# First attention of a two-layer kernel: another order of the matrix groups within a segment

## The chip, the cores and the metric

The kernel runs on one core of a Trainium2 chip. A core has a matrix engine (TensorE, PE in the profile), three engines for elementwise work (VectorE or DVE, ScalarE or ACT, GpSimd or POOL), a queue that issues transfers (SyncE, SP) and 16 DMA engines. Every engine works through its own queue of instructions in order; semaphores tie the queues together. The metric is the device time of one execution, in microseconds.

## The reference

The program computes two gated layers: `x = x + attention(norm(x)) * silu(ffn(norm(x)))`, twice, on `x` of 4 batches x 512 tokens x 128. The change touches only the first attention, a recurrent one with a memory. With 16 heads of 64 and segments of 64 tokens, cut to what matters:

```python
def step(carry, seg):
    M, Z = carry                               # memory and its normaliser, per head
    q, k, v = ...                              # the segment's 64 tokens, per head
    scores = jnp.einsum('bhid,bhjd->bhij', q, k) * scale
    scores = jnp.where(mask, -jnp.inf, scores)
    att_dot = jnp.einsum('bhij,bhjv->bhiv', softmax(scores), v)
    sq = elu(q) + 1.0
    att_mem = sq @ M / (sq @ swapaxes(Z, -2, -1))
    sk = elu(k) + 1.0
    M_new = M + jnp.einsum('bhld,bhlv->bhdv', sk, v)
    Z_new = Z + sk.sum(axis=-2, keepdims=True)
    att = gate * att_mem + (1.0 - gate) * att_dot
    out = att.reshape(B, LSEG, H * DV) @ Wo
    return ((M_new, Z_new), out)
```

A batch has 8 segments, so there are 32 steps; the memory starts anew with each batch.

## The kernel before

The kernel runs, in this order: the norm and the FFN of the first layer, the first attention (`attn0`, lines 563 to 864), the FFN of the second layer, the second attention. Inside `attn0` the loop `for n in range(nseg)` (line 823) goes over the 32 segments n = 0 to 31. The statements of the loop body fix the order on each engine: what is called earlier stands earlier in the queue of every engine that it uses (only transfers may be issued somewhat earlier or later). The work is software pipelined: while segment n is finished, the scores, keys and queries of n + 1 are prepared and the attention of n - 1 is transposed. The steps, with the tile names that the profile shows:

- `elu_exp(n, w)`: ScalarE takes the exponential (`elu`) and the relu (`up`) of the keys (w = 1) or queries (w = 0) of a segment. `elu(n, w)` (line 679): VectorE makes `min(elu, 1) + up` of them; all three tiles lie in SBUF.
- `scores(n)`: 16 matmuls of 64x64, one per head, spread over the four 64x64 quadrants of TensorE, into PSUM `sc`; VectorE caps and masks them into `E` (line 656). `scores_exp(n)`: ScalarE takes their exponential.
- `memory(n)`: 16 quadrant matmuls of the queries' elu with the memory `mz`, into `mm`; VectorE divides (`rm`, `t`, lines 711 and 712); GpSimd multiplies by the gate (line 731).
- `update(n)`: 16 quadrant matmuls of the keys with the values (`vone`), into `mu`; VectorE adds them to the memory (line 746). It is left out in the last segment of a batch (n % 8 = 7).
- `keys(n)`: four transposes of 128x128 into `pk`; ScalarE copies them to `sk`. It is left out for n % 8 = 7.
- `attend(n)`: 16 quadrant matmuls of `E` with the values, into `dot`; VectorE divides (lines 765, 711, 712) and keeps the largest sums (`sums`, line 768); GpSimd multiplies by the other gate (line 769) and adds the memory's part (line 770).
- `attended(n)`: four transposes into `pa`; ScalarE copies them to `attT` in four instructions.
- `output(h)`: 64 matmul halves into `po` for every four segments, at n % 4 = 1; VectorE multiplies by the gate (line 802), GpSimd adds to `x` (line 803).
- `project(h)`: twelve chunks that make the queries, keys and values of the four segments of group h: eight of q and k (`pp`, 8 matmuls each with 64 columns, evicted by ScalarE to `pj`), four of v (`pv`, evicted to `vt` by ScalarE, by VectorE for the first two groups, and sent to DRAM `vd` by SP). `todo` holds the chunks that are left; `each` of them, four in n = 0 to 2 and three later, are done in a segment, and none from n = 27 on. `values(n)`: SP loads `vone` back from `vd`, two segments ahead.
- `between`: FFN steps of the second layer that are slipped in from n = 18 on.

PSUM has two rings: `wide` (tag `w`, three buffers of two banks), which scores, memory, update, attend and output take in turn, and `narrow` (tag `t`, two buffers of one bank), which chunks, `pk` and `pa` take in turn. A group can start when the buffer that it takes has been evicted. `E`, `elu`, `vt` and the `pj` tiles have two buffers each, `vone` four.

Of the kernel before, what the change touches and what calls it, by code (L numbers as in the profile page):

```python
# [107 lines left out]
class Kernel:  # L108
# [454 lines left out]
    def attn0(self, xnT, g0, stack, psum, between):  # L563
# [25 lines left out]
        def wide(name):  # L589

            return psum.tile([P, 2, S], F32, name=name, tag="w", bufs=3)

        def narrow(name):
            return psum.tile([P, S], F32, name=name, tag="t", bufs=2)
# [44 lines left out]
        def blocks(n, w):  # L639
            s = n % 4  # L640
            return qkv[n // 4][w][:, s * 8 : s * 8 + 8, :]
# [20 lines left out]
        def scores_exp(n):  # L662
            e = seg[n]["e"]
            self.act1(e, e, AF.Exp, scale=1.0 / math.sqrt(DK))

        def last(n):
            return n % 8 == 7

        def elu_exp(n, w):
            t = pool.tile([P, 8, 64], F32, name=f"elu{w}{n}", tag=f"elu{w}")  # L670
            up = pool.tile([P, 8, 64], F32, name=f"up{w}{n}", tag="up")
            self.act1(t, blocks(n, w), AF.Exp)
            self.act1(up, blocks(n, w), AF.Relu)
            seg[n][w] = t, up

        def elu(n, w):

            t, up = seg[n][w]
            self.vec1(nc.vector.scalar_tensor_tensor(t, t, 1.0, up, ALU.min, ALU.add))  # L679
            seg[n][w] = t  # L680

        def turn(n, src, name):

            ps = narrow(f"{name}{n}").rearrange("p (hp c) -> p hp c", hp=4)
            for hp in range(4):
                self.pin(nc.tensor.transpose(
                    ps[:, hp], src[:, 2 * hp : 2 * hp + 2, :].rearrange("d a j -> d (a j)"),
                    self.ident,
                ))
            return ps.rearrange("p hp (x d) -> p hp x d", x=2)  # L690

        def keys(n):
            t = pool.tile([P, 4, 2, DK], F32, name=f"sk{n}", tag="sk")
            self.act1(t, turn(n, seg[n][1], "pk"), AF.Copy)
            seg[n]["sk"] = t

        def values(n):

            for p in range(2):
                src = vd[n // 4][p].rearrange("(s hp r) d -> s r hp d", s=4, hp=4)  # L700
                nc.sync.dma_start(out=vone[n % 4][:, :, p, 0:DK], in_=src[n % 4])

        def heads(ps):

            return ps[:, :, 0 : 4 * (DK + 1)].rearrange("p x (y v) -> p x y v", v=DK + 1)

        def over(t):
            return t.rearrange("p (x hp) y d -> p x (hp y) d", x=2)

        def divided(ps, t, r, sums):  # L710
            self.vec1(nc.vector.reciprocal(r, sums))
            self.vec1(nc.vector.tensor_tensor(t, heads(ps)[:, :, :, 0:DK], bc(r, 3, DK), ALU.mult))  # L712

        def memory(n):


            mz, sq = self.mz[(n % 8 + 1) % 2 + 1 if n % 8 else 0], seg[n][0]
            ps = wide(f"mm{n}")
            for hp in range(4):
                for p in range(2):  # L720
                    for a in range(2):
                        at = (2 * a + hp // 2) * (DK + 1)
                        self.mm1(
                            ps[halves[(a + hp) % 2], p, at : at + DK + 1],
                            lhsT=sq[halves[p], 2 * hp + a, :], rhs=mz[halves[p], hp, a, :],
                            start=True, stop=True,
                        )
            t = seg[n]["t1"] = pool.tile([P, 4, 2, DK], F32, name=f"t1{n}", tag="t1")
            r = pool.tile([P, 2, 4], F32, name=f"rm{n}", tag="rm")
            divided(ps, t.rearrange("p hp y d -> p y hp d"), r, heads(ps)[:, :, :, DK])  # L730
            nc.gpsimd.tensor_mul(t, t, self.gate)  # L731
# [16 lines left out]
        def attend(n):  # L748


            e, v = seg[n]["e"], vone[n % 4]
            ps = wide(f"dot{n}")
            for u in range(2):
                for p in range(2):
                    for hp in (2 * u, 2 * u + 1):
                        for a in range(2):
                            at = (2 * u + p) * (DK + 1)
                            self.mm1(
                                ps[halves[(a + hp) % 2], a, at : at + DK + 1],
                                lhsT=e[halves[a], p, hp, :], rhs=v[halves[a], hp, p, :],  # L760
                                start=True, stop=True,
                            )
            both = pool.tile([P, 2, 2, 4], F32, name=f"rd{n}", tag="rd")
            sums = both[:, 0]
            self.vec1(nc.vector.tensor_scalar_max(sums, heads(ps)[:, :, :, DK], SUM_MIN / 2))
            t = pool.tile([P, 4, 2, DK], F32, name=f"t2{n}", tag="t2")
            divided(ps, over(t), both[:, 1], sums)
            self.vec1(nc.vector.tensor_tensor(self.sums0, both, self.sums0, ALU.max))  # L768
            nc.gpsimd.tensor_mul(t, t, gate2)  # L769
            nc.gpsimd.tensor_add(t, t, seg[n]["t1"])  # L770
            seg[n]["att"] = t

        def attended(n):

            if n % 4 == 0:

                attT[n // 4] = pool.tile([P, 16, 4, 32], F32, name=f"attT{n}", tag="attT")
            ps = narrow(f"pa{n}").rearrange("p (hp c) -> p hp c", hp=4)
            for hp in range(4):
                self.pin(nc.tensor.transpose(  # L780
                    ps[:, hp, :], seg[n]["att"][:, hp].rearrange("i p v -> i (p v)"),
                    self.ident,
                ))
            src = ps.rearrange("p (a u) (h t c) -> p c a u h t", a=2, h=2, c=16)
            dst = attT[n // 4][:, :, n % 4].rearrange("p c (u y t) -> p c u y t", u=2, y=4)
            for h in range(2):
                for a in range(2):
                    self.act1(dst[:, :, :, (a + h) % 2 * 2 + a], src[:, :, a, :, h], AF.Copy)

        def output(h):  # L790
            ps = wide(f"po{h}")
            for c in range(16):
                for p in range(2):
                    self.mm1(
                        ps[:, p, 0:D], lhsT=attT[h][halves[p], c].rearrange("v s x -> v (s x)"),
                        rhs=self.wo[halves[p], c, :],
                        start=(c == 0), stop=(c == 15),
                    )
            two = slice(h * 2, h * 2 + 2)
            gate = g0[h // 2][:, h % 2 * 2 : h % 2 * 2 + 2, :]  # L800
            sg = pool.tile([P, 2, D], F32, name=f"sg{h}", tag="sg")
            self.vec1(nc.vector.tensor_tensor(sg, ps[:, :, 0:D], gate, ALU.mult))
            nc.gpsimd.tensor_add(self.x[:, two, :], self.x[:, two, :], sg)
# [4 lines left out]
        todo = project(0)  # L808
# [14 lines left out]
        for n in range(nseg):  # L823
            if n == 0 or n % 4 == 3:
                todo = project((n + 1) // 4 + 1)
                each = 3 if n else 4
            nxt = n + 1 < nseg
            more = nxt and not last(n + 1)
            if n + 2 < nseg:
                values(n + 2)  # L830
            if more:
                elu_exp(n + 1, 1)
            if nxt:
                scores(n + 1)
            if n % 4 == 1 and n > 4:
                output(n // 4 - 1)
            for chunk in todo[:1]:
                chunk()
            if more:
                elu(n + 1, 1)  # L840
            if nxt:
                scores_exp(n + 1)
            memory(n)
            for chunk in todo[1:2]:
                chunk()
            if nxt:
                elu_exp(n + 1, 0)
            if not last(n):
                update(n)
            if nxt:  # L850
                elu(n + 1, 0)
            for chunk in todo[2:each]:
                chunk()
            todo = todo[each:]
            if more:
                keys(n + 1)
            for f, *args in between.get(n - 0.5, []):
                f(*args)
            attend(n)
            if n:  # L860
                attended(n - 1)
            for f, *args in between.get(n, []):
                f(*args)
        return [lambda: attended(nseg - 1), lambda: output(2 * B - 1)]
# [1392 lines left out]
```

## Time and profile before

| | us |
|---|---|
| three runs | 774.92, 775.71, 767.96 |
| median | 774.92 |
| the profiled execution | 772.95 |
| its span, first to last instruction | 771.1 |
| first attention's loop up to n = 27, 93.66 to 310.09 | 216.43 |
| n = 27 to the last memory group, 310.09 to 335.54 | 25.45 |

| engine | busy in the whole span | busy in 93.66 to 310.09 | busy in 310.09 to 335.54 |
|---|---|---|---|
| PE | 729.7 | 210.29 | 20.06 |
| DVE | 522.8 | 141.68 | 20.86 |
| ACT | 489.6 | 155.23 | 14.97 |
| POOL | 292.7 | 111.68 | 17.05 |

The mean granted clock of TensorE is 0.981. How the profile is read: it shows one execution. Times count from the span's start. In a timeline each row is a run of equal instructions: its start, how long it lasted, engine, line, operation, the tiles written and read, shapes, and how many; a bracket gives the idle time of the engine just before and what ended it. Matmuls are pipelined, so the end of a group of matmuls overlaps the start of the next; the distance between two starts is the time that a group takes. L331 is a helper through which nearly all matmuls go, and L334 one for ScalarE, so groups are told apart by their tiles.

### The profile page before, as it was taken

Reading aid. Unit: us, or ns where it says so; the run is one execution under the profiler, and the core shown is the slowest. Engines: PE = TensorE matmul, PEld = TensorE weight load, DVE = VectorE, ACT = ScalarE, POOL = GpSimd, SP = SyncE. Lnnn points to the kernel's source line nnn. Section 1 sums busy time; section 2 is a strip of 40 time slices with the busy share of each in tenths; the row PEclk is TensorE's granted clock in tenths of the full one; section 3 lists DMA queues with packets and bytes.
Section 4 is the critical chain, followed back from the end, with each engine's and each line's share of the span. In section 5 each row is a group of like instructions: output and inputs, shape, how many; then the busy total and the mean of one; then the engine's idle time right before and its main releaser. Section 6 shows DMA issues by size and latency. Waiting matters only on the chain. (4 is left out here: it accounts for less than half of the span.)

```text
span 771.1 us, 23617 instructions
## 1 busy us (share of the span) xinstructions
PE 729.7 (95%) x10060; PEld 439.4 (57%) x10060; DVE 522.8 (68%) x1133; ACT 489.6 (63%) x793; POOL 292.7 (38%) x340
## 2 busy tenths in 40 slices
PE   8999899999999989889999998999999999999996
PEld 4665677787876858767677775333233433432235
DVE  7776375657558755774356633798897799857864
ACT  4432566768667776653332224899897879889940
POOL 7660045555555435563045030231441244130250
PEclk9999999999999999999999999899999999999997
DMA  7830423223123121100003710849676766749200
GB/s 194 145 84 0 111 85 98 69 61 94 44 75 98 31 83 31 31 3 1 1 0 105 220 47 1 197 153 207 134 210 157 162 140 187 199 113 212 55 16 17
DMA packets 77743, 74.71 MB, mean 97 GB/s; under 512 B 41936, under 2 KB 66800, under 8 KB 74560
## 3 DMA queue, kind: packets, MB, share of 16 engines
q1 hardware_dynamic: 75568, 71.98, 36.0%
q0 software_dynamic: 1488, 0.90, 0.8%
q8 instruction: 81, 1.33, 0.8%
q10 hardware_dynamic: 576, 0.26, 0.1%
q14 instruction: 30, 0.25, 0.1%
HBM read 50.04 MB, written 23.07 MB: 95 GB/s over the span
## 5 line engine op out<-in xcount | busy, mean ns | idle before, releaser
L334 ACT ACTIVATE e<-s 128x1024 f32<-128x1024 f32 x126 | 123.1, 1042 | 24.7 <-PE s L331 23.9
L331 PE MATMUL acc<-e,strip 128*32 128x512 f32 x1008 | 124.9, 604 | 0.3 <-DVE e L1692 0.3
L334 ACT ACTIVATE e<-e 128x1024 f32<-128x1024 f32 x100 | 103.1, 1080 | 0.0
L334 ACT ACTIVATE h<-ph 128x1024 f32<-128x1024 f32 x32 | 32.8, 1025 | 84.2 <-PE ph L331 84.2
L769 POOL TENSOR_TENSOR t<-t,gate 128x512 f32<-128x512 f32 x32 | 40.9, 1277 | 72.3 <-DVE sums L768 64.2
L331 PEld LDWEIGHTS eo<-w_out,h 128*128 128x128 f32 x512 | 60.7, 192 | 12.5 <-issue 9.7
L331 PEld LDWEIGHTS acc<-e,strip 128*32 128x32 f32 x1008 | 28.7, 109 | 68.3 <-issue 59.2
L331 PE MATMUL eo<-w_out,h 128*128 128x128 f32 x512 | 63.4, 277 | 1.6 <-DVE g L966 1.4
L334 ACT ACTIVATE pj<-pp 128x512 f32<-128x512 f32 x64 | 38.3, 598 | 39.9 <-PE pp L331 39.4
L679 DVE SCALAR_TENSOR_TENSOR elu<-elu,up 128x512 f32<-128x512 f32 x60 | 48.5, 808 | 20.4 <-ACT up L334 20.4
L331 PE MATMUL ph<-xnT,w_in 128*128 128x512 f32 x128 | 60.3, 594 | 0.0
L731 POOL TENSOR_TENSOR t<-t,gate 128x512 f32<-128x512 f32 x32 | 41.5, 1297 | 40.2 <-DVE t L712 40.1
L966 DVE SCALAR_TENSOR_TENSOR g<-eo,gw,g 128x128 f32<-128x128 f32 x112 | 31.4, 343 | 36.3 <-PE eo L331 36.3
L770 POOL TENSOR_TENSOR t<-t,t 128x512 f32<-128x512 f32 x32 | 46.0, 1438 | 2.5
L331 PE MATMUL s<-q,k 64*128 64x512 bf16 x256 | 41.1, 389 | 5.8 <-DVE g L966 3.5
L1692 DVE TENSOR_TENSOR e<-e 128x1024 f32<-128x1024 f32 x26 | 34.5, 1327 | 15.2 <-ACT e L334 15.2
L331 PEld LDWEIGHTS <-k 64*128 64x128 bf16 x256 | 8.2, 94 | 62.8 <-issue 60.2
L1543 POOL TENSOR_TENSOR pr<-pr,pr 128x512 f32<-128x512 f32 x14 | 20.6, 1489 | 49.6 <-DVE pr L1538 49.6
L334 ACT ACTIVATE elu<-pj 128x512 f32<-128x512 f32 x60 | 38.0, 634 | 0.1
L334 ACT ACTIVATE up<-pj 128x512 f32<-128x512 f32 x60 | 37.9, 631 | 0.0
L334 ACT ACTIVATE attT<-pa 128x128 f32<-128x128 f32 x128 | 25.1, 283 | 18.7 <-PE pa L780 18.7
L331 PE MATMUL pv<-l0Wv,xnT 128*128 128x512 f32 x64 | 35.5, 652 | 0.8 <-ACT vt L334 0.7
(291 smaller groups left out, 1538.5 us busy)
## 6 DMA issues: line engine op xcount, KB each, us to landing
vd<-vt SPq DMA_DIRECT2D x32, 256.0 KB
vone<-vd SPq DMA_DIRECT2D x64, 128.0 KB
first<-qe SPq DMA_DIRECT2D x8, 1024.0 KB
second<-qf SPq DMA_DIRECT2D x16, 512.0 KB
third<-qf SPq DMA_DIRECT2D x32, 256.0 KB
qf<-qT SPq DMA_DIRECT2D x64, 64.0 KB
k<-kd SPq DMA_DIRECT2D x16, 256.0 KB
q<-qd SPq DMA_DIRECT2D x16, 256.0 KB
```

The lines of the kernel that those rows point to most:

```text
L331: return self.pin(self.nc.tensor.matmul(*args, **kw))
L334: return self.pin(self.nc.scalar.activation(*args, **kw))
L679: self.vec1(nc.vector.scalar_tensor_tensor(t, t, 1.0, up, ALU.min, ALU.add))
L731: nc.gpsimd.tensor_mul(t, t, self.gate)
L769: nc.gpsimd.tensor_mul(t, t, gate2)
L770: nc.gpsimd.tensor_add(t, t, seg[n]["t1"])
L966: self.vec1(v.scalar_tensor_tensor(acc[b][:, k, :], eo[:, k, :], w, acc[b][:, k, :], ALU.mult, ALU.add))
L1543: self.nc.gpsimd.tensor_add(self.prod1[b, m], self.prod1[b, m], t)
L1692: self.vec1(self.nc.vector.tensor_mul(t, src[pair], src[pair]))
```

## The change

Only the order of the calls in the loop body changes. `memory(n)` moves up to stand right behind `scores(n + 1)`. `output` moves behind the first chunk and `scores_exp`. `update(n)` and `attend(n)` follow each other, `keys(n + 1)` comes after them and just ahead of `attended(n - 1)`. `elu_exp(n + 1, 0)` and `elu(n + 1, 0)`, the queries' part for the next segment, move from the middle to after `attended(n - 1)`, and all chunks but the first move to the end of the segment.

```diff
                 elu_exp(n + 1, 1)
             if nxt:
                 scores(n + 1)
-            if n % 4 == 1 and n > 4:
-                output(n // 4 - 1)
+            memory(n)
             for chunk in todo[:1]:
                 chunk()
             if more:
                 elu(n + 1, 1)
             if nxt:
                 scores_exp(n + 1)
-            memory(n)
-            for chunk in todo[1:2]:
-                chunk()
-            if nxt:
-                elu_exp(n + 1, 0)
+            if n % 4 == 1 and n > 4:
+                output(n // 4 - 1)
             if not last(n):
                 update(n)
-            if nxt:
-                elu(n + 1, 0)
-            for chunk in todo[2:each]:
-                chunk()
-            todo = todo[each:]
-            if more:
-                keys(n + 1)
             for f, *args in between.get(n - 0.5, []):
                 f(*args)
             attend(n)
+            if more:
+                keys(n + 1)
             if n:
                 attended(n - 1)
+            if nxt:
+                elu_exp(n + 1, 0)
+                elu(n + 1, 0)
+            for chunk in todo[1:each]:
+                chunk()
+            todo = todo[each:]
             for f, *args in between.get(n, []):
                 f(*args)
```

On TensorE a segment with three chunks ran `sc pp mm pp mu pp pk dot pa` before, and runs `sc mm pp mu dot pk pa pp pp` after. On VectorE it was E, elu of the keys, the memory's division, the update's addition, elu of the queries, attend's steps; it becomes E, the memory's division, elu of the keys, the update's addition, attend's steps, elu of the queries. On ScalarE the exponential and relu of the queries stood ahead of the last chunk's eviction, `sk` and `attT`; they stand behind `attT` and ahead of the evictions of the last chunks. GpSimd's order stays, but for the addition of `output`, which comes behind the gate product of the memory.

## The prediction

> I read the timeline first, because the page gives only averages (PE 95%, DVE 68%, ACT 63%): the change touches one stage, 93 to 335 us, 32 segments n = 0 to 31.
>
> **What bounds the kernel now.** TensorE's timeline of one segment, n = 10 (start us, duration us, engine, line, operation):
>
> ```profile
> 171.06 0.69 PE L331 MATMUL sc<-pj,pj 64*64 64x64 f32 x32
> 171.69 1.09 PE L331 MATMUL pp<-xnT,l0Wq 128*64 128x128 f32 x16
> 172.71 0.70 PE L331 MATMUL mm<-mz,elu 64*64 64x65 f32 x32
> 173.34 1.09 PE L331 MATMUL pp<-xnT,l0Wq 128*64 128x128 f32 x16
> 174.36 0.70 PE L331 MATMUL mu<-vone,sk 64*64 64x65 f32 x32
> 174.99 1.09 PE L331 MATMUL pp<-xnT,l0Wq 128*64 128x128 f32 x16
> 176.01 0.66 PE L686 MATMUL pk<-ident,elu 128*128 128x128 f32 x4
> 176.60 0.70 PE L331 MATMUL dot<-vone,E 64*64 64x65 f32 x32
> 177.22 0.66 PE L780 MATMUL pa<-ident,t 128*128 128x128 f32 x4
> 177.81 0.69 PE L331 MATMUL sc<-pj,pj 64*64 64x64 f32 x32
> ```
>
> Each group starts before the one ahead ends, none shows an idle time: TensorE sets the period, 177.81 - 171.06 = 6.75 us. A group's slot is the distance of starts: quadrant group 0.63, projection chunk 1.02, transposes 0.59. At n = 27 no chunks are left, and quadrant groups stand side by side:
>
> ```profile
> 310.09 0.69 PE L331 MATMUL sc<-pj,pj 64*64 64x64 f32 x32
> 310.60 0.65 PE L331 MATMUL mm<-mz,elu 64*64 64x65 f32 x32
> 311.07 0.66 PE L331 MATMUL mu<-vone,sk 64*64 64x65 f32 x32
> ```
>
> Slots of 0.51 and 0.47 instead of 0.63. That is the size of the saving on offer: about 0.15 for a quadrant group followed by its like, 0.07 for a chunk (two chunks at 105.35 take 1.90, not 2.04), 0.10 for transposes (0.49, at 263.60).
>
> The second thing to read is VectorE beside GpSimd, at n = 27 and 28:
>
> ```profile
> 312.05 0.69 DVE L679 SCALAR_TENSOR_TENSOR elu<-elu,up 128x512 f32<-128x512 f32 x1 [0.50 <-ACT up L334]
> ...
> 313.83 1.28 POOL L731 TENSOR_TENSOR t<-t,gate 128x512 f32<-128x512 f32 x1
> ...
> 314.17 1.49 DVE L679 SCALAR_TENSOR_TENSOR elu<-elu,up 128x512 f32<-128x512 f32 x1
> ...
> 316.84 1.27 POOL L769 TENSOR_TENSOR t<-t,gate 128x512 f32<-128x512 f32 x1 [1.73 <-DVE sums L768]
> 317.30 1.36 DVE L679 SCALAR_TENSOR_TENSOR elu<-elu,up 128x512 f32<-128x512 f32 x1
> ...
> 318.19 1.60 POOL L770 TENSOR_TENSOR t<-t,t 128x512 f32<-128x512 f32 x1
> ```
>
> The elu step costs 0.69 alone, but 1.49 or 1.36 when it starts during a GpSimd product: it ends 0.55 after that product's end (315.66 against 315.11, 318.66 against 318.11; the same 0.55 in every such pair of the stage). And L770, whose turn came while elu ran, took 1.60 instead of 1.28. [...] In the steady segments (n = 10) elu of the queries runs at 176.14, when GpSimd is idle (L731 ended at 176.09); that is what the change moves.
>
> [...]
>
> **The change, part by part.** No instruction or byte is added or removed; groups are reordered on four queues.
>
> *TensorE, gain.* A three-chunk segment becomes sc mm | pp | mu dot | pk pa | pp pp: five mode changes instead of nine. Slots: 0.48 + 0.63 + 1.02 + 0.48 + 0.63 + 0.49 + 0.59 + 0.95 + 1.02 = 6.29, so 0.46 saved if nothing waits. Over the stage 97 changes of mode go, about 0.13 each: 12.6 us at most.
>
> *The narrow PSUM pair (tag t, two buffers), loss.* The chunk after pk and pa takes pk's buffer, which the sk eviction frees: pk to sk start 0.69, sk 0.60, so pk + 1.34 instead of pk + 1.08. TensorE alone: 6.29 + 0.26 = 6.55. The wide ring's order (sc, mm, mu, dot) is the same, its releases come earlier.
>
> *The queries' elu, loss.* On ScalarE elu_exp(n+1, 0) now stands behind sk and the four attT copies, and on VectorE elu(n+1, 0) behind attend's last step; next segment's mm waits for it, and behind mm on TensorE wait a chunk, mu, dot, pk; behind elu on VectorE wait E, rm, t1. From the start of dot:
> ScalarE: dot to pk 0.63; to sk 0.69; sk to attT 0.50; attT to the exponential 0.645; to the relu 0.53; to elu 0.67. elu could start at dot + 3.66.
> GpSimd: mu is 0.48 before dot, so mz (mu + 0.76) starts at dot + 0.28, rd 0.61 later at 0.89, L769 1.27 after rd (178.63 - 177.36) at 2.16, L770 1.36 later (179.99 - 178.63) at 3.52, ending at 4.80.
> elu arrives 0.14 after L770 has begun. [...] elu ends at 4.80 + 0.55 = 5.35. mm starts 0.13 later (315.66 to 315.78/315.81): 5.48. From mm to dot: 0.63 + 1.02 + 0.48 = 2.13. **Period 7.61, against 6.75.** TensorE, at 6.55, waits 1.06 per segment. Arrivals 0.00 to 0.33 after a product's start do not occur in this trace (0.33 is the least, and blocked), so this is bounded from both sides: if elu wins, it ends at 4.35, mm is at 4.48, and the period is 6.61.
>
> The keys' elu now follows t1 at once and starts 0.26 before L731 would (t1 + 0.61 against t1 + 0.87): it wins, L731 ends 0.4 to 0.6 later than alone, with over 0.6 spare before L769. pk at mm + 2.76 is after elu's end (mm + 2.36).
>
> Undisturbed segments, mm to mm after against sc to sc before:
> n = 10, 18, 26: 7.61 - 6.75 = 0.86, three times: 2.6. n = 4, 8, 12, 16, 20 (a value chunk first, 1.05): 7.64 - 6.78 = 0.86: 4.3. n = 3, 11: 7.64 - 6.69: 1.9. n = 5, 9, 13, 17, 25 (with output, 3.77): 11.38 - 10.84 = 0.54 (before, po also waits 0.3 for attT): 2.7. n = 7, 15 (no update): 7.04 - 6.30: 1.5. n = 1, 2 (four chunks): 7.61 against 7.6: 0.
> n = 6, 14: no pk; elu comes at dot + 3.18, during L769, ends 3.99. But the last query chunk is now the last group, and next segment's sc reads it: pa at dot + 0.63, chunks at 1.21 and 2.16, eviction from 3.31 to 3.91, sc, mm at 4.44: 6.57 - 6.16: 0.8.
> Sum 13.8.
>
> *Where the trace is disturbed* (n = 19, 21 to 24: FFN items, a clock dip at 285 to 288, a 0.88 wait at 246): between 0 and 0.86 each; I take 0.3: 1.5. *Start*: at n = 0, 1 VectorE evicts the value chunks; these now stand behind elu, and the fourth waits for a vt buffer, so for a DMA: 0 to 3.3, I take 2.5. *End*, n = 27 to 31, no chunks to hide anything: mm to mm 6.3, 6.3, 10.3 (po) and 5.5 by the same chain, 28.4 against 334.92 - 310.60 = 24.3: 4, between 1 and 6.
>
> *At nothing.* SP: vd<-vt of the second and third value chunk issues a few us later; its first reader, the vone load of segment n + 2 at n = 6, 10, ..., is two segments off, which hides it; without that, one landing. The vone loads wait for dot of two segments before, as now. GpSimd's order stays; pa(n-1) needs L770(n-1), done at dot + 5 of a period over 6.5 long. The output group, now behind the first chunk, hides inside its own 3.77.
>
> Sum: 13.8 + 1.5 + 2.5 + 4 = 21.8. Against the profiled execution's 772.95 us (span 771.1): 794.7, I say **794**. The median of the three runs is 2 higher, the lowest 5 lower.
>
> **Rivals.** *Elu wins the port* (17 in 100). The decision is 0.14 us wide; [...] the period is 6.61: n = 3, 4, 8, 11, 12, 16, 20 and 26 together gain about 1, the output segments 0.46 each (2.3), n = 7, 15 gain 0.2; n = 10, 18 lose 0.6 each and n = 6, 14 0.8, as sc waits for the last query chunk; start and end lose 1.5 and 3. Net +3: 776, no change that can be told.
> *The drains decide* (13 in 100). If ScalarE and GpSimd run earlier than I chain them, so that neither port nor sk's buffer holds TensorE, 12.6 us of drains and the 0.3 us waits of six po groups (1.9) go: 758.5. For it: TensorE is gapless today. Against it: the sk eviction alone costs 0.26 by rows of this trace. It decides if elu is ready by about dot + 3.4, 0.26 earlier than worked out: then it enters between L769 and L770.
> *Not done as said*: the instruction order of the changed kernel on each engine is the order used above, so no chance is given.
>
> **From cases to numbers.** Port lost 0.70: 794, own range 785 to 800 (the ends of start, end and disturbed segments). Port won 0.17: 770 to 779. Drains 0.13: 755 to 765. Range 775 to 800 leaves out the drains, part of port won and a little of the first. Slower by over 1% (what a measurement can tell) 0.70, within 1% 0.17, faster 0.13.
>
> **What would show it.** Right: elu<-elu,up of the queries at 1.7 to 2.1 us instead of 0.69, ending 0.55 after L770; TensorE idle some 1 us before mm, put down to elu; sc to mm and mu to dot at 0.5. Wrong: elu at 0.69 after the sums step with L770 at 1.60 (port won); no idle before mm (drains); or a wait for vone or vt on SP, which I priced at nothing.

## The result, and the profile after

The changed kernel takes 800.62 us (median of six runs, 799.23 to 802.69) against 774.78 for the kernel before on the same chip (six runs, 767.96 to 775.71): a ratio of 1.0353, 95% interval 1.0314 to 1.0392. It is slower, as predicted, and 6.6 us above the predicted 794. By the medians the change costs 25.8 us, where 21.8 were forecast; the rest of the 6.6 is that the forecast was added to one execution of 772.95, below the median, and rounded down.

The profiled execution of the changed kernel took 802.69 us (span 800.9), 2.1 above its median; that of the kernel before took 772.95 (span 771.1), 1.8 below its own. The two traces therefore differ by 29.8 us of span, more than the medians, and the accounts below are made against 29.8.

TensorE's timeline of a steady segment after the change, n = 8 (start us, duration us, engine, line, operation, idle time ahead of it and what ended it):

```profile
161.53 0.70 PE L331 MATMUL mm<-mz,elu 64*64 64x65 f32 x32 [0.38 <-DVE elu L679]
162.15 1.12 PE L331 MATMUL pv<-l0Wv,xnT 128*128 128x512 f32 x2
163.21 0.70 PE L331 MATMUL mu<-vone,sk 64*64 64x65 f32 x32
163.72 0.65 PE L331 MATMUL dot<-vone,E 64*64 64x65 f32 x32
164.30 0.66 PE L686 MATMUL pk<-ident,elu 128*128 128x128 f32 x4
164.79 0.60 PE L780 MATMUL pa<-ident,t 128*128 128x128 f32 x4
165.64 1.97 PE L331 MATMUL pp<-xnT,l0Wk 128*64 128x128 f32 x32 [0.25 <-ACT sk L334]
167.54 0.69 PE L331 MATMUL sc<-pj,pj 64*64 64x64 f32 x32
169.08 0.70 PE L331 MATMUL mm<-mz,elu 64*64 64x65 f32 x32 [0.84 <-DVE elu L679]
```

The slots did shrink: mu to dot is 0.51, pk to pa 0.49, and two chunks side by side take 1.90. Two waits that were not there before eat this and more: 0.25 ahead of the second chunk, for the eviction of `sk` (predicted 0.26), and 0.84 ahead of `mm`, for the queries' elu. From mm to mm it is 7.55 us, where the prediction has 7.61 to 7.64.

VectorE and GpSimd in the same segment:

```profile
165.85 1.27 POOL L769 TENSOR_TENSOR t<-t,gate 128x512 f32<-128x512 f32 x1 [0.80 <-DVE sums L768]
...
167.19 1.28 POOL L770 TENSOR_TENSOR t<-t,t 128x512 f32<-128x512 f32 x1
167.32 1.70 DVE L679 SCALAR_TENSOR_TENSOR elu<-elu,up 128x512 f32<-128x512 f32 x1 [1.54 <-ACT up L334]
```

The elu is released 0.13 us after GpSimd's addition has started, and takes 1.70 instead of 0.69. It ends at 169.02, 0.55 after the addition's end at 168.47, and `mm` follows 0.06 later. Not every segment goes this way. At n = 1, 19, 20, 24, 27 and 30 elu starts 0.01 to 0.07 ahead of the addition, takes 0.69, and it is the addition that is longer, as at n = 19:

```profile
261.13 0.69 DVE L679 SCALAR_TENSOR_TENSOR elu<-elu,up 128x512 f32<-128x512 f32 x1 [1.35 <-ACT up L334]
261.19 1.78 POOL L770 TENSOR_TENSOR t<-t,t 128x512 f32<-128x512 f32 x1
```

In the page's list of the costliest groups (busy us, mean ns of one; then idle time ahead, and what ended it) the loss is seen as a sum; the first line is of the kernel before, the others of the changed kernel:

```profile
L679 DVE SCALAR_TENSOR_TENSOR elu<-elu,up 128x512 f32<-128x512 f32 x60 | 48.5, 808 | 20.4 <-ACT up L334 20.4
...
L679 DVE SCALAR_TENSOR_TENSOR elu<-elu,up 128x512 f32<-128x512 f32 x60 | 60.7, 1011 | 48.9 <-ACT up L334 48.9
L331 PE MATMUL mm<-mz,elu 64*64 64x65 f32 x1024 | 23.7, 232 | 21.2 <-DVE elu L679 21.0
```

The elu's mean rises from 808 to 1011 ns, and TensorE stands idle for it 21.0 us in all. TensorE's share of the span falls from 95% to 91%.

The end of the loop is where the prediction was least right. TensorE from n = 28 on, some groups left out:

```profile
334.50 0.94 PE L331 MATMUL mm<-mz,elu 64*64 64x65 f32 x32 [2.15 <-DVE elu L679]
335.15 1.16 PE L331 MATMUL mu<-vone,sk 64*64 64x65 f32 x32
...
342.21 1.15 PE L331 MATMUL mm<-mz,elu 64*64 64x65 f32 x32 [2.85 <-DVE elu L679]
343.29 6.28 PE L331 MATMUL po<-l0wo,attT 64*128 64x128 f32 x64
...
355.45 1.15 PE L331 MATMUL mm<-mz,elu 64*64 64x65 f32 x32 [3.13 <-DVE elu L679]
...
361.82 1.02 PE L331 MATMUL mm<-mz,elu 64*64 64x65 f32 x32 [2.72 <-DVE elu L679]
```

All four waits are for elu, as in the steady segments, and longer, because no chunk is left to fill them. GpSimd's addition is not always in it: ahead of the first and the last of these groups elu starts 0.05 and 0.04 us before the addition (333.67 and 360.98) and takes 0.69, so there its late place alone costs the time. But the matmul groups themselves are longer too: 1.15 for 0.70, 1.16 for 0.70, and the output group 6.28 for the 3.84 that it takes elsewhere. The granted clock is 0.86 from 320 to 345 us and 0.79 from 345 to 370; it was 0.99 from 94 to 320. Read in half microseconds from 320 to 370 it is 1.00 or 0.50, but for the steps between them: 0.50 from 334.8 to 338.2, 341.6 to 348.5, 355.3 to 358.7 and 362.1 to 365.5. This was not in the prediction, but the kernel before shows it at the same place, from 318.9 to 322.3:

```profile
318.71 0.96 PE L686 MATMUL pk<-ident,elu 128*128 128x128 f32 x4 [1.06 <-DVE elu L679]
319.60 1.15 PE L331 MATMUL dot<-vone,E 64*64 64x65 f32 x32
```

So the 24.3 us of the kernel before, from which the prediction starts, already hold one such stretch.

The account of the 29.8 us, with the prediction's own terms (memory group to memory group after, against scores to scores before, as the prediction did; the end from memory group to memory group in both):

| part | predicted | measured |
|---|---|---|
| undisturbed segments, n = 3 to 18, 20, 25, 26 | 13.8 | 12.6 |
| n = 1, 2 | 0 | 1.8 |
| disturbed segments, n = 19, 21 to 24 | 1.5 | 0.7 |
| n = 0 | 2.5 | 1.9 |
| end, memory group of n = 27 to that of n = 31 | 4 (1 to 6) | 9.3 |
| past the memory group of n = 31 | not priced | 2.9 |
| seams (start of the loop, and n = 27) | 0 | 0.7 |
| sum | 21.8 | 29.9 |

### The profile page after: what moved, and what is told of

It is laid out like the page before. It is cut to its first block, busy times and chain, and to the rows that moved or that the text cites. A ratio compares the mean times of both kernels' runs of the same rounds, so it can differ in the third digit from the quotient of the medians.

```text
span 800.9 us, 23571 instructions
## 1 busy us (share of the span) xinstructions
PE 727.9 (91%) x10060; PEld 441.3 (55%) x10060; DVE 532.5 (66%) x1133; ACT 483.9 (60%) x793; POOL 295.1 (37%) x340
## 5 line engine op out<-in xcount | busy, mean ns | idle before, releaser
L331 PE MATMUL acc<-e,strip 128*32 128x512 f32 x1008 | 126.9, 614 | 0.3 <-DVE e L1689 0.3
L679 DVE SCALAR_TENSOR_TENSOR elu<-elu,up 128x512 f32<-128x512 f32 x60 | 60.7, 1011 | 48.9 <-ACT up L334 48.9
L731 POOL TENSOR_TENSOR t<-t,gate 128x512 f32<-128x512 f32 x32 | 50.3, 1573 | 100.5 <-DVE t L712 100.5
L334 ACT ACTIVATE pj<-pp 128x512 f32<-128x512 f32 x64 | 36.6, 611 | 29.5 <-PE pp L331 29.4
L769 POOL TENSOR_TENSOR t<-t,gate 128x512 f32<-128x512 f32 x32 | 40.7, 1273 | 31.1 <-DVE sums L768 28.1
L334 ACT ACTIVATE sk<-pk 128x512 f32<-128x512 f32 x28 | 16.7, 596 | 50.8 <-PE pk L686 50.8
L331 PE MATMUL mm<-mz,elu 64*64 64x65 f32 x1024 | 23.7, 232 | 21.2 <-DVE elu L679 21.0
```

Source lines behind the costliest of these rows:

```text
L331: return self.pin(self.nc.tensor.matmul(*args, **kw))
L334: return self.pin(self.nc.scalar.activation(*args, **kw))
```

## The experiments

The theory is that of the prediction: the elu arrives just behind GpSimd's addition (by 0.13 us) and has to wait for it (1.70 instead of 0.69). The recorded texts call what the two wait for the port; that there is one thing that both need was the author's assumption, and the traces show the waits alone. Drains and changes of mode stand there for the longer slot of a matrix group beside one of another kind, 0.63 against 0.47 to 0.51 for quadrant groups; what makes it longer is not shown. The theory's rivals: that elu's place in the queues costs the time, whichever of the two goes first; and, for the end, that the chain through elu was reckoned too short, against a fall of TensorE's clock. All times are medians, with the ratio to runs of the kernel before on the same chip. On these chips the kernel before took 771.4 to 774.8 us, so two runs of different chips are compared by their ratios, turned into us at 772.

### Elu and the addition: take an operation away ahead of the addition

```diff
-            nc.gpsimd.tensor_mul(t, t, gate2)
```

> The changed kernel without the gate product of the attention on GpSimd (1 - gate is not applied, 32 products of 1.28 us are left out). Port theory: the addition then runs where the product ran, from dot + 2.2 to dot + 3.4, and is over when the queries' elu comes at dot + 3.66; elu 0.69, period about 6.6, time 776 to 785, as with the pause. Rival, place alone: GpSimd is not on TensorE's path, 798 to 801.

The kernel leaves out the factor 1 - gate. Measured: 785.88 us, ratio 1.0186 (1.0166 to 1.0206), some 13 us below the changed kernel, and 0.9 above the upper end of what the theory expected. The addition (line 769 here) now starts earlier and is just over when elu comes. Of this kernel's trace, n = 19:

```profile
249.09 1.28 POOL L769 TENSOR_TENSOR t<-t,t 128x512 f32<-128x512 f32 x1 [0.68 <-DVE sums L768]
...
250.36 0.69 DVE L679 SCALAR_TENSOR_TENSOR elu<-elu,up 128x512 f32<-128x512 f32 x1 [1.35 <-ACT up L334]
...
251.11 0.70 PE L331 MATMUL mm<-mz,elu 64*64 64x65 f32 x32
```

The addition ends at 250.37, elu starts at 250.36, takes 0.69, and no idle time is shown before `mm`; mm to mm is 6.70 (244.41 to 251.11). Elu stands in the same place of every queue as in the changed kernel, so in these segments the place alone does not cost the time.

### Elu and the addition: hold the addition back, first try

```diff
+        pause = pool.tile([P, 64], F32, name="pause", bufs=1)
             nc.gpsimd.tensor_mul(t, t, gate2)
+            self.pool1(nc.gpsimd.memset(pause, 0.0))
```

> The changed kernel with one GpSimd memset of 128x64 (about 0.2 us) added between the gate product of the attention (L769 of the changed kernel) and the addition (L770), 32 times. Port theory: the queries' elu comes 0.12 after the addition's start in the changed kernel; with the pause it comes first, so it takes 0.69 instead of 1.70, the period of a three-chunk segment falls from 7.5 to about 6.6, and the time falls by 16 to 22 us, to 779 to 785, although work is added. Rival, place in the queues alone (the elu is late on ScalarE and VectorE, the port does not matter): no gain, 800 to 803.

Measured: 797.57 us, ratio 1.0335 (1.0306 to 1.0364): no gain. The trace says why, and it is not that the theory is wrong:

```profile
184.72 1.28 POOL L770 TENSOR_TENSOR t<-t,gate 128x512 f32<-128x512 f32 x1 [0.78 <-DVE sums L769]
...
185.94 0.16 POOL L771 MEMSET pause<- 128x64 f32 x1
...
186.08 1.26 POOL L772 TENSOR_TENSOR t<-t,t 128x512 f32<-128x512 f32 x1
186.21 1.68 DVE L680 SCALAR_TENSOR_TENSOR elu<-elu,up 128x512 f32<-128x512 f32 x1 [1.55 <-ACT up L334]
```

The memset starts 0.06 before the product ends at 186.00. The addition starts 1.36 after the product, just as without it (1.34 in n = 8 above). Hardly anything was shifted, elu still came 0.13 late, and the run tells nothing of the theory.

### Elu and the addition: hold the addition back, with a longer memset

```diff
-        pause = pool.tile([P, 64], F32, name="pause", bufs=1)
+        pause = pool.tile([P, 512], F32, name="pause", bufs=1)
```

> The changed kernel with a memset of 128x512 on GpSimd between the gate product and the addition of attend. A memset of 128x64 there lasted 0.16 us and began before the product had ended, so the addition still began 0.13 ahead of the queries' elu. Nothing is left out. A memset of 128x768 takes 0.74 us in the trace, so this one should take about 0.5 and the addition should begin some 0.35 later, 0.2 behind elu's arrival. Port theory: elu then takes 0.69 in nearly all steady segments, a three-chunk segment has a period of 6.6 instead of 7.55, and the time is 776 to 787, though GpSimd has more to do. If the memset itself holds the port until it ends, elu waits for that and takes about 1.0, with the same verdict. Rival, the place of elu in the queues and not the port: period and time stay, 797 to 802.

Measured: 784.79 us, ratio 1.0143 (1.0123 to 1.0163). The kernel has half a microsecond more GpSimd work in each segment than the changed kernel and is some 16 us faster:

```profile
183.34 1.28 POOL L770 TENSOR_TENSOR t<-t,gate 128x512 f32<-128x512 f32 x1 [0.73 <-DVE sums L769]
...
184.56 0.53 POOL L771 MEMSET pause<- 128x512 f32 x1
184.82 0.69 DVE L680 SCALAR_TENSOR_TENSOR elu<-elu,up 128x512 f32<-128x512 f32 x1 [1.54 <-ACT up L334]
185.04 1.62 POOL L772 TENSOR_TENSOR t<-t,t 128x512 f32<-128x512 f32 x1
```

Now elu comes 0.22 ahead of the addition. It takes 0.69, and it is the addition that is longer, 1.62 instead of 1.28. The segments n = 3, 8, 11 and 12 take 6.50 to 6.56, where the prediction has 6.61 for the case that elu wins; n = 10, 18 and 26, whose scores wait for the last query chunk, as in the one shown, take 7.28 or 7.29 instead of 7.51 or 7.52. At n = 7 and 15 the memset does the reverse: elu starts 0.23 behind the addition, takes 1.60, and the segment grows from 6.90 to 7.25 and 7.24. This settles it: with all queues in the changed kernel's order, it is the one of the two that starts second that is longer, here elu 0.69 and the addition 1.62, in the changed kernel elu 1.70 and the addition 1.28. What elu did during the memset is of use too: it started 0.26 behind the memset's start, 0.27 ahead of its end, and took 0.69, so this memset did not hold it up.

### Elu and the addition: elu well ahead of it

```diff
                 scores(n + 1)
+                elu_exp(n + 1, 0)
...
                 update(n)
+            if nxt:
+                elu(n + 1, 0)
...
-            if nxt:
-                elu_exp(n + 1, 0)
-                elu(n + 1, 0)
```

> The changed order with the queries' exponential and relu moved to the head of the segment, beside the keys', and their elu behind the update; the matrix groups stay as changed. If the late elu is what costs, the drains show: TensorE is held only by the sk eviction (pk + 1.34) and, every fourth segment, by the eviction of the last query chunk ahead of the scores; period about 6.55, 764 to 774. If the pairing itself costs (PSUM rings), it stays near 800.

Measured: 767.71 us, ratio 0.9949 (0.9930 to 0.9969). The loop keeps the changed kernel's order on TensorE and loses the wait before `mm`, as at n = 4:

```profile
125.21 0.69 PE L331 MATMUL sc<-pj,pj 64*64 64x64 f32 x32
125.72 0.65 PE L331 MATMUL mm<-mz,elu 64*64 64x65 f32 x32
```

Most segments of three chunks take 6.48 to 6.50. Elu does not run undisturbed here: in most segments it starts during the memory's gate product and takes 1.12 to 1.17, but no group waits for it. So the late elu, with what hangs on it, was the difference between slower and slightly faster. The 0.25 for `sk` stays, and so does the slower start: from the memory group of n = 0 to that of n = 3 it is 24.57 us, against 23.12 before.

At its end this trace has two arrivals closer behind an addition's start than the 0.33 that the prediction knew:

```profile
314.57 1.82 POOL L770 TENSOR_TENSOR t<-t,t 128x512 f32<-128x512 f32 x1
314.58 0.68 DVE L679 SCALAR_TENSOR_TENSOR elu<-elu,up 128x512 f32<-128x512 f32 x1
...
319.48 1.28 POOL L770 TENSOR_TENSOR t<-t,t 128x512 f32<-128x512 f32 x1
319.54 1.77 DVE L679 SCALAR_TENSOR_TENSOR elu<-elu,up 128x512 f32<-128x512 f32 x1
```

At 0.01 behind the addition's recorded start elu still goes first, at 0.06 it waits. In all traces of this case no elu that came 0.06 or more behind such a start went first.

### The end: the old order for the last five segments

The loop body of the changed kernel stands in the first branch, that of the kernel before in the second:

```diff
+            if n < 27:
...
+            else:
...
```

> The changed order for n = 0 to 26, the order of before for n = 27 to 31. If the end of the stage is the mis-sized term (33.6 us from the memory group of n = 27 to that of n = 31 in the changed kernel, 24.3 before), this gives 8 to 10 us back: 791 to 793. If the excess over the forecast lies elsewhere (start, segments with FFN items), it gives back the 4 us that the forecast put there: 796 to 797.

Measured: 788.11 us, ratio 1.0216 (1.0192 to 1.0241), some 11 below the changed kernel by the ratios, a little more than the 8 to 10 expected if the end is the cause, and far from the 4 of the other case. In its trace memory group to memory group from n = 27 to 31 takes 22.2 us (327.25 to 349.43), and what follows 436.6 against 439.1. The table has 9.3 + 2.9 = 12.2 for the end, so the end is where the prediction's miss sits. The 24.3 of the kernel before hold a stretch of 3.4 us at 0.50; the 22.2 here hold none (1.00 from 320 to 370 us).

### The end: keep TensorE busy during the waits

```diff
+        def warm(n):
+            ps = narrow(f"wm{n}")
+            for k in range(4):
+                self.mm1(ps, lhsT=xnT[3][:, 0, :], rhs=self.wqkv[2][:, 0:S], start=True, stop=True)
...
+            if n >= 27:
+                warm(n)
             memory(n)
```

> The changed kernel with four extra value-projection matmuls (128x512, nobody reads them) between the scores and the memory group for n = 27 to 31, in the time that TensorE waits for elu there. Clock theory: the waits of 2 to 3 us let TensorE's granted clock fall, so that po takes 6.3 instead of 3.8 and the quadrant groups 0.9 to 1.1 instead of 0.5; with TensorE kept busy these go back to their lengths, 3 to 6 us less: 795 to 798. Rival: the clock is not what makes the end long, the elu chain alone is: no change, or up to 2 us more where the filler outlasts the wait.

Measured: 799.84 us, ratio 1.0377 (1.0359 to 1.0396): no gain. In its trace the clock does stay up (output group 3.84, memory groups 0.70), but the four matmuls take 3.70 us where the wait was 2.15 to 3.13. The memory groups of n = 28 and 29 come 7.71 and 7.70 behind the one before them; in the changed kernel it was 6.29 and 7.71. The filler gave away what the clock brought. Half as much of it is the better test:

```diff
-            for k in range(4):
+            for k in range(2):
```

> The changed kernel with two extra value matmuls of 128x512 (instead of the four of the run before, whose 3.7 us outlasted the waits of 2.2 to 3.1) on TensorE between the scores and the memory group from n = 27 on; their result is not read. They take about 1.9 us, less than any of the waits for elu at n = 28 to 31. Clock theory (the end of the loop costs more than predicted because TensorE's granted clock falls during the waits): the output group at n = 29 is back at 3.84 from 6.28, the memory groups of n = 27 to 31 lie about 28.5 apart instead of 33.6, and the time falls by 4 to 6 to 795 to 797. Rival (the chain through elu alone is longer at the end than reckoned): 33 stays, 800 to 802.

Measured: 796.59 us, ratio 1.0304 (1.0272 to 1.0336), 4 below the changed kernel. The two intervals overlap by a little, so the trace has to carry the verdict:

```profile
335.43 0.70 PE L331 MATMUL mm<-mz,elu 64*64 64x65 f32 x32
...
341.63 0.70 PE L331 MATMUL mm<-mz,elu 64*64 64x65 f32 x32
342.25 3.84 PE L331 MATMUL po<-l0wo,attT 64*128 64x128 f32 x64
...
351.88 0.70 PE L331 MATMUL mm<-mz,elu 64*64 64x65 f32 x32 [1.13 <-DVE elu L686]
...
357.40 0.70 PE L331 MATMUL mm<-mz,elu 64*64 64x65 f32 x32 [1.58 <-DVE elu L686]
```

All groups are back at full speed, and the clock is 1.00 from 320 to 370 us. The memory groups of n = 27 to 31 lie 6.21, 6.20, 10.25 and 5.52 apart, 28.2 in all; the prediction's chain had 6.3, 6.3, 10.3 and 5.5. So the chain through elu was right to a tenth, and the other 5.4 of the changed kernel's 33.6 is the clock. The stretch past n = 31 is back as well, 435.9 us against 439.1 (before: 436.2); of this the half clock from 362.1 to 365.5 explains 1.7 at most, half its length, and the cause of the rest stays open. The filler itself costs 1.8 at n = 27, where there was no wait to hide it (9.30 instead of 7.52), which is one reason why the median falls by less.

### Each pair alone, in the order before

Memory right behind the scores, all else as before:

```diff
                 scores(n + 1)
+            memory(n)
...
                 scores_exp(n + 1)
-            memory(n)
```

> The kernel before with one thing changed: the memory group right behind the scores. Drain theory: a quadrant group followed by its like saves 0.15 and the two chunks that come together 0.07, about 0.2 in each of some 25 segments: 5 us less, 768 to 771. Rival: the memory group, earlier by a chunk, meets its elu or the memory's addition and waits: no gain or a loss, 774 to 785.

Measured: 764.13 us, ratio 0.9900 (0.9872 to 0.9929), better than expected. Most segments of three chunks save 0.15 to 0.36 where 0.2 was expected, and those with the output group 0.62 (10.22 for 10.84). The other pair, update right ahead of attend:

```diff
-            if not last(n):
-                update(n)
...
                 f(*args)
+            if not last(n):
+                update(n)
             attend(n)
```

> The kernel before with one thing changed: the update right ahead of the attention's group. Drain theory: 0.2 in each of some 25 segments: 768 to 771. Rival: the memory's addition comes later and the next memory group or the attention's division waits: 774 to 785.

Measured: 769.74 us, ratio 0.9984 (0.9958 to 1.0009): no difference that can be told. Its steady segments are shorter (6.44 instead of 6.75), but the memory groups of n = 20 to 31 lie 92.0 apart instead of 86.7, which in this execution takes all of it back. In that stretch its clock is at 0.50 for 17.1 us in all, against 6.8 in the kernel before, which could account for most of it; what brings it down more often was not tested.

### A version that beats both

Both pairs, transposes together, but elu where it has cover: exponential and elu of the queries ahead of the last chunk, which with the output now stands before update and attend; `vt` gets four buffers instead of two.

```diff
-                t = pool.tile([P, S], F32, name=f"vt{h}_{p}_{k}", tag="vt")
+                t = pool.tile([P, S], F32, name=f"vt{h}_{p}_{k}", tag="vt", bufs=4)
...
                 elu(n + 1, 1)
+                elu_exp(n + 1, 0)
+            for chunk in todo[1:2]:
+                chunk()
...
                 scores_exp(n + 1)
+                elu(n + 1, 0)
+            for chunk in todo[2:each]:
+                chunk()
+            todo = todo[each:]
             if n % 4 == 1 and n > 4:
...
-            if nxt:
-                elu_exp(n + 1, 0)
-                elu(n + 1, 0)
-            for chunk in todo[1:each]:
-                chunk()
-            todo = todo[each:]
```

> A new order with the same two pairs: sc mm, all chunks, update, attention, keys, attended; the queries' exponential stands behind the first chunk, so that sk and attT are evicted while sc and mm run, and vt has four buffers. If the costs are the ones named (late elu, sk's buffer, last query chunk), none is left: 6.2 us for a three-chunk segment and 9.9 with output, 757 to 764, faster than both kernels. If a wait that I don't see takes their place: 770 or more.

Measured: 754.22 us, ratio 0.9789 (0.9735 to 0.9842), the fastest of all. A part of segment n = 10:

```profile
166.94 2.89 PE L331 MATMUL pp<-xnT,l0Wq 128*64 128x128 f32 x48
...
168.12 1.43 DVE L679 SCALAR_TENSOR_TENSOR elu<-elu,up 128x512 f32<-128x512 f32 x1
...
169.74 1.50 DVE L679 SCALAR_TENSOR_TENSOR elu<-elu,up 128x512 f32<-128x512 f32 x1 [0.19 <-ACT up L334]
```

Both elus still start during a GpSimd operation and take 1.43 and 1.50 instead of 0.69. It costs nothing here, since three chunks and two quadrant groups run ahead of `pk`, the first reader: the keys' elu ends 1.30 ahead of `pk`, the queries' 1.18 ahead of the next `mm`. The segment takes 6.06 us.

The same without the extra buffers of `vt`:

> The best order so far (754.2 us: scores and memory side by side, then a chunk, elu of the keys, the queries' exponential, a chunk, scores' exponential, elu of the queries, the other chunks, output, update and attend side by side, keys and attended side by side) without the two extra buffers of vt. If the extra vt buffers matter, because the value chunks of n = 0 and 1 wait for a transfer, it is 2 to 3 us slower than with them, 756 to 758. If not, 753.5 to 755.

Measured: 764.05 us, ratio 0.9864 (0.9817 to 0.9911): by the ratios some 6 us slower than with them, where 2 to 3 were expected. The two intervals overlap a little, and the four runs spread from 759.87 to 767.46, with the profiled one the slowest. The steady segments are the same (6.06, 6.16). The traces part at the start (mm of n = 0 to mm of n = 3, 23.4 against 23.0, after a start that is 2.5 later in this execution) and above all at n = 21 to 24, where value chunks and FFN steps meet; from n = 20 to n = 25 it is 51.1 us against 44.9. Of these 6.2 us, 4.3 lie at n = 23, where TensorE waits 1.08 and 2.67 us for evictions into `vt`. Its clock falls behind the second of these (0.90 from 250 to 300 us, 1.00 with four buffers). Another 1.6 lie at n = 21, where the clock falls behind a wait of 1.76 for `pj` that both kernels have; that part is not shown to come from `vt`.

## Why the prediction was right in kind and short in size

*The queries' elu, loss.* Right. The arrival 0.14 behind the addition measured 0.13, the end 0.55 behind the addition's end measured 0.55, the period 7.61 measured 7.50 to 7.57. That elu waits for the addition, the choice the forecast hung on, is shown by the long memset and by the product left out: each has elu no longer wait for the addition, and they bring some 16 and 13 us.

*The narrow PSUM pair.* Right, 0.25 to 0.29 for 0.26 where a chunk follows `sk`.

*Undisturbed segments.* 12.6 for 13.8. With the output group it was 11.31 for 11.38; n = 7 and 15 took 6.90 for 7.04, n = 6 and 14 6.80 for 6.57. Two of them came near their number by luck: at n = 16 `pa` waits 0.62 for an eviction into `vt` that a transfer holds up, a wait that the prediction put at nothing, and at n = 20 elu goes ahead of the addition, but FFN steps on VectorE hold up the keys' elu, and `pk` waits 0.81 for it.

*n = 1, 2, priced at 0.* Wrong, 1.8. With four chunks the last one ends the segment. At n = 2 it waits 0.22 for a chunk's eviction, then the scores wait 0.70 for its own, as the prediction worked out for n = 6 and 14 but did not apply here. Elu is over by then: it ends at 120.30, and the scores start at 120.94. At n = 1 the last chunk waits 0.23, and `pk` 0.54 for the keys' elu.

*Start.* 1.9 for 2.5, and only in part by the cause given. VectorE's evictions stand behind elu, as said, and the fourth value chunk waits 1.67 us for them; VectorE's own wait for a buffer of `vt`, 1.55 until 105.02, comes after that chunk. Another 0.81 is lost ahead of `pk`, which waits for the keys' elu; the prediction doesn't have this.

*End, n = 27 to 31: 4, between 1 and 6.* **This is the step that failed.** It measured 9.3, and 2.9 more past n = 31. The chain of 28.4 was right (28.2 with TensorE kept busy); what was left out is that TensorE's granted clock, with waits of 2.15 to 3.13 us in these segments, fell to half (0.50), which cost 5.4 within them and up to 1.7 behind them. What the other 1.2 or so behind them are stays open. The wait ahead of each group was worked out, and the step then took the groups at their full-speed durations, though `dot` at 319.60 in the kernel before had taken 1.15 for 0.70 in this very stage.

*The rivals.* That elu goes first was held open because no arrival under 0.33 was known. The traces now put the change-over between 0.01 and 0.06 behind the addition's recorded start, so 0.13 was on the losing side; the long memset shows the other period (6.5 for 6.61). Its time, 776, was too low for a kernel in that state: 784.79 with the memset. There the loop's start (3.5 more from n = 0 to n = 3) and end (28.4 against 24.3) stay, and the clock falls again at n = 30. That the shorter slots decide is not what happened here, but the saving exists once elu is out of the way: 0.9900 with one pair alone.

## What to carry to other kernels

Before moving an elementwise step on VectorE, list where GpSimd's operations will stand at its new arrival; if the two are within tenths of a microsecond (0.13 here), the order is the risk, and a longer step costs nothing only where other work lies before its reader (as for the 1.43 and 1.50 of the fastest version). When a wait on TensorE is worked out at 2 us or more and comes again in each turn of a loop, as the waits of 2.15 to 3.13 here, don't take the matmuls behind it at full speed: price the same segment at both clocks, and look whether the trace of before has a slow group in that stage. A reordering of several groups is best split: one of the two pairs alone brought 1%, all of it together cost 3.5%.

## What was not expected of the hardware

*TensorE's clock fell though no single wait was over 3.13 us.* In the changed kernel's trace it fell to 0.50, and dot took 1.12 to 1.16 for 0.65. The four slow stretches at the end last 3.4 or 6.8 us and begin 6.8, 13.7 and 6.8 us apart; from the first to the last it is 27.3 us, eight times 3.41. In the 3.41 us ahead of the four falls TensorE was busy for 37, 34, 13 and 20%. In the kernel with the long memset the waits of 2.15 ahead of 326.15 and 332.44 brought no fall; counted in steps of 3.41 from that trace's own falls, each lies across the border of two steps, and the four steps are busy for 61, 48, 50 and 68%. The clock falls there after steps of 43 and 20%. So the length of a wait alone did not decide; that its place among such steps counts is the author's reading of these two traces, not tested by a run. The busy share alone doesn't decide either: among FFN steps the clock of the kernel before fell at 284.8 after 3.41 us that were busy for 82%, and the cause of that stays open. Waits of about 0.84 in the steady segments of the changed kernel did not bring a fall about (1.00 from 94 to 290 us).

*A short GpSimd instruction was nearly free.* A memset of 0.16 us between two GpSimd products moved the second by 0.02 (1.36 from product to addition instead of 1.34); one of 0.53 moved it by 0.36 (1.70).

*The loser's delay was constant.* Wherever elu came behind the addition in the changed kernel's steady segments, it ended 0.54 to 0.56 us after the addition's end (169.02 against 168.47, 187.85 against 187.30); where the addition lost, in the kernel with the long memset, it ended 1.15 after elu's end (186.66 against 185.51).
